# First item's x in whole rows, turned on the tensor engine; the adjacency compared later; the second item's products beside the first attention block

## The chip, the cores and the metric

The kernel runs on one core of a Trainium2 chip. The core has five engines that work side by side, each through its own list of instructions in order: PE (TensorE) multiplies matrices, DVE (VectorE) and POOL (GpSimd) do elementwise work, ACT (ScalarE) does functions and copies, SP issues transfers. Engines wait for one another by semaphores. The metric is device microseconds of one launch. The kernel before took 2934.19 us, the median of 4 runs (2933.64 to 2935.59).

## The reference

x has 32 items of 512 nodes by 512 features; adj is one 512 by 512 matrix of zeros and ones for all items. A masked attention with 8 heads of 64 is followed by a graph convolution, each with a residual and a layer norm:

```python
q, k, v = x @ Wq + bq, x @ Wk + bk, x @ Wv + bv          # per head of 64
scores = q k^T / sqrt(64) + where(adj == 0, -1e9, 0)
x = layernorm(x + softmax(scores) @ v)
norm_adj = adj * rsqrt(deg)[:, None] * rsqrt(deg)[None, :]   # deg = adj.sum(axis=1)
x = layernorm(x + norm_adj @ (x @ weight) + bias)
```

## The kernel before

**Work of one item.** The three products x Wv, x Wk, x Wq need x with its features on the partitions (tile XT). Each product of 2 by 2 blocks is made as seven block products instead of eight (function `seven`, the Winograd scheme): slots 0 to 3 of XT and of a weight tile are the plain blocks, and slots 4, 5, 6 and again 2 are differences or sums of them (`combine` for XT, `weigh` for a weight). A product of seven is called a piece below: PE multiplies a slot of XT with a slot of a weight into one of three PSUM tiles (`mm`, three buffers), and DVE adds it into the result. Pieces of the values come from `values_of(b)` (seven per item), pieces of keys and queries from `keys_and_queries(b, r)` (seven for r = 0, seven for r = 1). Pieces 1 and 2 read slots 0 and 1 of XT, piece 3 slot 5, piece 4 slot 6, piece 5 slot 4, pieces 6 and 7 slots 2 and 3.

**Attention** goes in four blocks per item, a block being two heads. A block has two halves; in each, `scores` multiplies keys and queries (tile sc, two PSUM buffers), DVE caps them and subtracts the mask (e<-sc,maskT), ACT takes the exponential in place, POOL adds the exponentials into acc (`accumulate`). One block later `values` multiplies them with v (tile av), and after every second block `sums` multiplies acc of two blocks with a selecting matrix sel, to get the row sums for all partitions.

**The order of the work is written out by hand.** The class InOrder (line 44, so nearly every instruction of the profile stands on L44) keeps every engine's instructions in the order of the program text. The main loop (line 704) runs over k, the blocks of all items. A turn of it puts out: the additions of acc left over from the block before (`pending`), the first half of the scores of block k, `values` of block k - 1, `sums` where k is even, the second half of the scores, and then one share of the next item's work (`shares`, made by `cut`, which counts pieces). For the first item the shares of k = 1 to 4 are 6, 5, 5 and 5 pieces; `degrees` (row sums of adj and their roots, DVE then POOL) and the four sums and differences of the last weight W1 (`w1_parts`, on POOL) lie between the pieces.

**The start.** x of an item is read in pieces of 32 elements (128 bytes) per row, so that DVE's transposition of 32 by 32 blocks (`turn`, two halves per item) gives XT. SP issues eight such transfers for item 0, then the biases, Wk, Wq, adj and W1; the queue of ACT issues Wv. Then follow the values of item 0 (7 pieces), its keys and queries (14 pieces), and between the last seven of these `adjacency(m)` for four m: PE transposes a block row of adj, and DVE makes the mask from it (maskT), copies it rounded (adjT), compares the two (off) and counts the differences (lost). After that comes `turn(1, 0)`, and the loop starts; the second half of item 1 is turned after the scores of block 0.

Of the kernel before, what the change touches and what calls it, by code (L numbers as in the profile page):

```python
# [9 lines left out]
F32 = mybir.dt.float32  # L10
# [3 lines left out]
AF = mybir.ActivationFunctionType  # L14
ALU = mybir.AluOpType
AX = mybir.AxisListType

P = 128
# [31 lines left out]
def unshifted(  # L50
# [54 lines left out]
    def load_x(b, j):  # L105


        if b == 0 and j == 1:
            X[b, j] = work.tile([P, 8, DT, 32], F32, name="x1", tag="e", bufs=6)
        else:  # L110
            X[b, j] = acts.tile([P, 8, DT, 32], F32, name="x", bufs=1)
        for q in range(4):
            nc.sync.dma_start(
                X[b, j][32 * q : 32 * (q + 1)],
                x[b, ts(j, HALF), ts(q, P)].rearrange("(k s) (t r) -> s k t r", s=32, r=32),
            )

    def turn(b, j):
        vector.transpose(
            XT[:, 2 * j : 2 * j + 2].rearrange("p i u (k s) -> p (i u) k s", s=32),  # L120
            X.pop((b, j)).rearrange("p k t r -> p t k r"),
        )
        if j == 0 and b:
            load_x(b, 1)

    def combine(b, at):
        to, a, c = ((4, 2, 0), (5, 3, 4), (6, 3, 2), (2, 5, 1))[at]
# [15 lines left out]
        for i in range(NT):  # L143
            nc.sync.dma_start(R[b][i], x[b, ts(i, P), :])

    def load_parts(w, name, engine):
        t = consts.tile([P, 7, 2, HALF], F32, name=name)
        for i in range(2):
            for q in range(4):
                engine.dma_start(  # L150
                    t[32 * q : 32 * (q + 1), 2 * i : 2 * i + 2].rearrange("r j u o -> r (j u) o"),
                    w[ts(q, P), ts(i, HALF)].rearrange("(t r) o -> r t o", r=32),
                )
        return t
# [7 lines left out]
    def weigh(t, engine):  # L162
        for at in range(4):
            weigh_part(t, engine, at)

    def load_row(v, name, engine):
        t = consts.tile([P, v.shape[0]], F32, name=name)
        engine.dma_start(t, bass.AP(tensor=v.tensor, offset=v.offset, ap=[[0, P], [1, v.shape[0]]]))
        return t

    def load_column(v, name):
        t = consts.tile([P, DT], F32, name=name)
        nc.sync.dma_start(t, v.rearrange("(t p) -> p t", p=P))
        return t

    load_x(0, 0)
    load_x(0, 1)
    wv = load_parts(Wv, "wv", nc.scalar)
    bv_r = load_row(bv, "bv_r", nc.scalar)
    bk_c = load_column(bk, "bk_c")  # L180
    bq_c = load_column(bq, "bq_c")
    wk = load_parts(Wk, "wk", nc.sync)
    wq = load_parts(Wq, "wq", nc.sync)
    adj_sb = acts.tile([P, NT, N], F32, name="yT")
    nc.sync.dma_start(adj_sb, adj.rearrange("(t p) o -> p t o", p=P))
    w1 = consts.tile([P, 7, 2, HALF], F32, name="w1")
    for i in range(2):
# [2 lines left out]
            W1[:, ts(i, HALF)].rearrange("(t p) o -> p t o", p=P),  # L190
        )
    b1_r = load_row(b1, "b1_r", nc.sync)

    ident = consts.tile([P, P], F32, name="ident")
    make_identity(nc, ident)
# [11 lines left out]
    dis = consts.tile([P, NT], F32, name="dis")  # L207
    lost = consts.tile([P, NT], F32, name="lost")

    def adjacency(m):  # L210


        p = ps_mm.tile([P, N], F32, name="mm")
        for n in range(NT):
            tensor.transpose(p[:, ts(n, P)], adj_sb[:, n, ts(m, P)], ident)
        vector.tensor_scalar(maskT[:, m, :], p, 0.0, FAR, op0=ALU.is_equal, op1=ALU.mult)
        vector.tensor_copy(adjT[:, m, :], p)
        off = work.tile([P, N], F32, name="off", tag="e", bufs=6)
        vector.tensor_tensor(off, p, adjT[:, m, :], ALU.not_equal)
        vector.tensor_reduce(lost[:, m : m + 1], off, AX.X, ALU.add)  # L220

    deg = consts.tile([P, NT], F32, name="deg")
    rdeg = consts.tile([P, NT], F32, name="rdeg")
# [109 lines left out]
    def turns(b):  # L333

        return [(0, turn, (b, 0))], [(0, turn, (b, 1))] + [(0, combine, (b, k)) for k in range(4)]
# [321 lines left out]
    def run(pieces):  # L657
        for _, f, args in pieces:
            f(*args)
# [22 lines left out]
    blocks = [(b, g) for b in range(B) for g in ORDER]  # L682
    S = len(blocks)
    weigh(wv, gpsimd)
    run(sum(turns(0), []))
    weigh(wk, gpsimd)
    scalar.activation(wq[:, :4], wq[:, :4], AF.Copy, scale=SCALE)
    first = values_of(0)
    run(first[:2])
    value_biases()  # L690
    biases()
    if B > 1:
        load_x(1, 0)
    run(first[2:])
    masks = [(0, adjacency, (m,)) for m in range(NT)]
    first = keys_and_queries(0, 0)
    run(first[:1])
    weigh(wq, vector)
    run(first[1:])
    run(weave(masks, keys_and_queries(0, 1)))  # L700
    one, two = turns(1)
    run(one)
# [1 line left out]
    for k in range(S + 1):  # L704
        b, at = divmod(k, G)
        if at == 1:
            if 0 < b < B - 1:
                load_residual(b - 1)
            if b + 2 < B:
                load_x(b + 2, 0)  # L710
            if b + 1 < B:
                main, kq = values_of(b + 1) + keys_and_queries(b + 1, 0), keys_and_queries(b + 1, 1)
                turn0, turn1 = turns(b + 2) if b + 2 < B else ([], [])
                main += kq[:5]
            if b == 0:
                w1_parts = [(0, weigh_part, (w1, gpsimd, i)) for i in range(4)]
                side = main[:7] + [(0, degrees, ())] + weave(w1_parts, main[7:]) + turn0 + kq[5:] + turn1
                shares = cut(side, (6, 5, 5, 5))
            elif b < B - 1:
                f, c = finish(b - 1), convolve(b - 1)  # L720
                norm, split, grow = f["norm"], f["split"], f["grow"]
                add, measure = f["add"], f["measure"]
                put_off = [(0, more, ())]


                beside = {
                    0: rest[:1], 1: rest[1:3], 2: put_off, 3: rest[3:4], 4: rest[4:5] + put_off,
                    5: rest[5:6] + f["inverse"], 6: rest[6:] + add[:2], 7: add[2:],
                    8: measure[:2] + put_off, 9: measure[2:], 10: f["root"] + put_off, 11: norm[:1],
                    12: norm[1:2] + split[:1], 13: norm[2:3] + split[1:2], 14: norm[3:] + split[2:3],  # L730
                    15: split[3:] + f["judge"], 16: put_off + grow[:2], 17: put_off + grow[2:], 18: turn0,
                }
                side = sum(([piece] + beside.get(i, []) for i, piece in enumerate(main)), [])
                side += c["first"] + c["parts"] + kq[5:] + turn1[:1]
                s = c["second"]
                if b < B - 2:
                    side += put_off + s[:1] + put_off + s[1:3] + turn1[1:2] + s[3:4] + turn1[2:3] + s[4:5]
                    side += turn1[3:4] + s[5:6] + c["measure"][:1] + turn1[4:] + s[6:] + c["measure"][1:2]
                    rest = c["measure"][2:] + c["root"] + c["store"]
                    shares = cut(side, (8, 8, 8, 8))  # L740
                else:
                    held, h, last = c, s, finish(b)
                    add = last["add"]
                    side += h[:1] + last["inverse"] + h[1:2] + add[:2] + h[2:3] + add[2:]
                    shares = cut(side, (8, 8, 8, 4))
            else:
                f, c, last = last, convolve(b - 1), finish(b)
                s, first, norm, split, add = c["second"], c["first"], f["norm"], f["split"], last["early"][1:]
                shares = [
                    h[3:4] + f["measure"][:2] + h[6:] + f["measure"][2:] + f["root"] + h[4:5] + f["judge"] + norm[:2]  # L750
                    + h[5:6] + split[:1] + norm[2:] + split[1:2],
                    split[2:] + last["early"][:1] + first[:1] + add[:2] + first[1:2] + add[2:] + first[2:]
                    + c["parts"] + f["grow"],
                    held["measure"] + held["root"] + s[:2] + held["store"],
                    [],
                ]


        while pending:
            more()  # L760
        if k == S - 2:
            load_residual(B - 1)
        if k < S:
            scores((*blocks[k], 0))
        if k:
            values((*blocks[k - 1], 0))
            values((*blocks[k - 1], 1))
            if k % 2 == 0:
                sums(blocks[k - 1][0], (k - 1) % G // 2)
        if k < S:  # L770
            accumulate((*blocks[k], 0))
            scores((*blocks[k], 1))
            if b == B - 1:
                accumulate((*blocks[k], 1))
            else:
                pending += [((*blocks[k], 1), (l,)) for l in range(2)]
        if k == S - G - 1:
            load_residual(B - 2)
        if k == 0:
            run(two)  # L780
        elif shares:
            run(shares.pop(0))

# [309 lines left out]
```

## Time and profile before

The profiled execution took 2933.54 us, its span is 2931.7 us, and the granted PE clock was 0.995 over it.

| | busy us | share |
|---|---|---|
| PE | 2872.2 | 98% |
| PE weight loads (beside PE) | 1882.8 | 64% |
| DVE | 2080.9 | 71% |
| ACT | 1057.2 | 36% |
| POOL | 1811.5 | 62% |

The page gives shares of the whole span. The change lies in the first 140 us, so what matters is read from the rows in order of time: the start, the duration, the engine, what is written from what, and in brackets how long the engine sat idle before it and what ended that. Matmuls overlap, so the step from one start to the next counts, not the duration of one. A float32 product is recorded as two matmuls. On PE the first piece starts at 9.48 us, the first scores at 56.87, and block 5 (the second block of item 1) at 134.10.

### The profile page before, as it was taken

How to read it: one execution, taken by the hardware profiler on the slowest of the kernel's cores; microseconds unless marked ns; L12 is line 12 of the kernel's file. 1: busy time of each engine (PE TensorE's matmuls, PEld its weight loads, DVE VectorE, ACT ScalarE, POOL GpSimd, SP SyncE). 2: the span in 40 equal slices, each digit the busy share in tenths (PEclk: the TensorE clock that was granted, in tenths of full speed). 3: DMA queues.
4: the chain of work that ended last, by engine and by line, in shares of the span. 5: the costliest groups of instructions: out<-in, count | busy, mean ns of one | idle time of the engine just before them, and what ended most of it. 6: DMA issues, size and time to landing. Idle time of an engine off the chain costs nothing.

```text
span 2931.7 us, 35519 instructions
## 1 busy us (share of the span) xinstructions
PE 2872.2 (98%) x12966; PEld 1882.8 (64%) x12966; DVE 2080.9 (71%) x2910; ACT 1057.2 (36%) x1340; POOL 1811.5 (62%) x1141
## 2 busy tenths in 40 slices
PE   7999999999999999999999999999999999999996
PEld 5666666666666666666666666666666666666654
DVE  7677766677666777666776667776667766777667
ACT  1233333343333433333432334333333333343343
POOL 2566666656666666666566666666566666656665
PEclk9999999999999999999999999999999999999998
DMA  5111122112221111211122211212111122111211
GB/s 130 33 26 47 47 58 53 38 37 51 54 54 42 40 49 47 58 42 39 47 51 54 55 40 36 53 49 55 43 40 47 48 57 54 40 37 48 58 33 52
DMA packets 383400, 142.42 MB, mean 49 GB/s; under 512 B 280048, under 2 KB 349680, under 8 KB 383216
## 3 DMA queue, kind: packets, MB, share of 16 engines
q1 hardware_dynamic: 381920, 138.75, 19.8%
q8 instruction: 104, 1.70, 0.2%
q10 hardware_dynamic: 1296, 1.31, 0.2%
q14 instruction: 80, 0.66, 0.1%
HBM read 72.88 MB, written 33.55 MB: 36 GB/s over the span
## 4 chain that ended last, share of the span: by engine, by line
PE 74%; DVE 16%; ACT 6%; issue 2%; POOL 2%; DMA 1%; SPq 0%; DVEq 0%; POOLq 0%; ACTq 0%
PE mm L44 47%; PE sc L44 15%; PE av L44 12%; DVE u L44 3%; ACT yT L44 3%; DVE e L44 3%; DVE st L44 3%; ACT hi L44 2%; DVE lo L44 2%; DVE low L44 1%; POOL rstd L44 1%; ACT e L44 1%; DVE mv L44 1%; DVE kq L44 1%; DVE v L44 1%
## 5 line engine op out<-in xcount | busy, mean ns | idle before, releaser
L44 ACT ACTIVATE e<-e 128x1024 f32<-128x1024 f32 x512 | 540.8, 1057 | 1096.5 <-DVE e L44 1077.8
L44 DVE SCALAR_TENSOR_TENSOR e<-sc,maskT 128x1024 f32<-128x1024 f32 x512 | 600.0, 1212 | 77.4 <-PE sc L44 76.9
L44 POOL TENSOR_TENSOR acc<-acc,e 128x1024 f32<-128x1024 f32 x248 | 597.3, 2408 | 64.3 <-ACT e L44 54.4
L44 PE MATMUL sc<-kq 64*128 64x512 f32 x2048 | 520.4, 622 | 17.1 <-DVE e L44 17.1
L44 POOL TENSOR_TENSOR acc<-e 128x1024 f32<-128x1024 f32 x126 | 296.9, 2356 | 382.3 <-ACT e L44 271.4
L44 PE MATMUL mm<-xT,wk 128*128 128x256 f32 x1792 | 469.6, 384 | 1.0 <-DVE off L44 1.0
L44 PE MATMUL av<-e,v 128*64 128x512 f32 x2048 | 467.7, 598 | 0.0
L44 PE MATMUL mm<-xT,wq 128*128 128x256 f32 x1792 | 459.9, 379 | 0.0
L44 PE MATMUL mm<-wv,xT 128*128 128x256 f32 x1792 | 407.5, 385 | 18.0 <-DVE xT L44 10.6
L44 PEld LDWEIGHTS mm<-xT,wk 128*128 128x128 f32 x1792 | 332.4, 190 | 113.5 <-issue 69.7
L44 PEld LDWEIGHTS mm<-wv,xT 128*128 128x128 f32 x1792 | 338.0, 192 | 93.6 <-issue 26.6
L44 PEld LDWEIGHTS mm<-xT,wq 128*128 128x128 f32 x1792 | 340.5, 190 | 46.3
L44 PEld LDWEIGHTS sc<-kq 64*128 64x128 f32 x2048 | 174.3, 186 | 301.5 <-issue 172.7
L44 PEld LDWEIGHTS av<-e,v 128*64 128x64 f32 x2048 | 135.6, 136 | 315.9 <-issue 315.2
L44 DVE TENSOR_TENSOR kq<-u,mm 128x512 f32<-128x512 f32 x128 | 87.9, 687 | 238.1 <-PE mm L44 238.0
L44 POOL TENSOR_TENSOR yT<-yT,xr 128x512 f32<-128x512 f32 x124 | 193.4, 1588 | 80.6 <-DVE yT L44 80.6
L44 PE MATMUL mm<-w,zT 128*128 128x256 f32 x992 | 224.5, 379 | 0.0
L44 POOL TENSOR_TENSOR rstd<-ve,minus_half 128x4 f32<-128x4 f32 (+1 forms) x65 | 65.5, 1008 | 252.9 <-DVE nmu L44 252.8
L44 POOL TENSOR_TENSOR yT<-yT,b_r 128x512 f32<-128x512 f32 x124 | 170.1, 1381 | 59.6 <-DVE lo L44 59.6
L44 PEld LDWEIGHTS mm<-w,zT 128*128 128x128 f32 x992 | 188.3, 190 | 26.3 <-issue 0.8
L44 PE MATMUL mm<-adjT,hi 128*128 128x512 f32 x496 | 201.9, 407 | 0.0
L44 PE MATMUL mm<-adjT,lo 128*128 128x512 f32 x496 | 196.1, 395 | 0.2 <-DVE lo L44 0.2
(123 smaller groups left out, 3177.7 us busy)
## 6 DMA issues: line engine op xcount, KB each, us to landing
x<-in_x_dram SPq DMA_DIRECT2D x256, 128.0 KB, 2.9
out_dram<-y SPq DMA_DIRECT2D x128, 256.0 KB, 2.1
xr<-in_x_dram SPq DMA_DIRECT2D x124, 256.0 KB, 3.6
yT<-yb SPq DMA_DIRECT2D x496, 64.0 KB, 2.5
wv<-in_L_gnn_Wv_dram ACTq DMA_DIRECT2D x8, 128.0 KB, 4.7
wk<-in_L_gnn_Wk_dram SPq DMA_DIRECT2D x8, 128.0 KB, 4.0
wq<-in_L_gnn_Wq_dram SPq DMA_DIRECT2D x8, 128.0 KB, 4.6
yT<-in_adj_dram SPq DMA_DIRECT2D x1, 1024.0 KB, 6.7
```

The source lines that it names most:

```text
L44: return self.tc.keep_in_program_order(op(*args, **kwargs))
```

## The change

- Item 0 of x is read first, as four transfers of 128 whole rows each (`load_residual(0)`, which was issued after the loads of the next item, at 26.55 us, and is needed later as the residual in any case). `turn_first(j)` makes half of XT from it on PE: 32 float32 products, each of 32 columns of the rows with the identity, into 32 partitions of a scores tile; the copy into XT is split between DVE (first quarter) and ACT (second). DVE's two `turn`s of item 0 and their eight transfers of 128-byte runs are gone.
- The second half of Wv goes on SP's queue behind x, Wk comes before the two bias columns. Both halves of item 1's x are issued before the loop, the second into one of the e buffers.
- Pieces 1 and 2 of the values of item 0 are put beside the turning, then DVE's four `combine`s. The four `weigh` steps of Wq lie between the first pieces of keys and queries.
- `adjacency` keeps only maskT on DVE; ACT copies adjT and an unrounded copy plainT. Comparison and counting (`compare(m)`) move into the shares of k = 3 and 4.
- The second half of item 1 is turned right after the first half of the scores of block 0, and five pieces of item 1's values are put into block 0: two after the first half of the scores, three after the second. The shares of k = 1 to 4 become 4 pieces each, and `degrees` follows the last two pieces of the values, in the share of k = 1.

```diff
+    def turn_first(j):
+        p = ps_sc.tile([P, 2, 2, HALF], F32, name="sc")
+        for i in range(2):
+            for u in range(2):
+                for n in range(2):
+                    for q in range(4):
+                        at = q * P + (2 * i + u) * 32
+                        tensor.matmul(
+                            p[32 * q : 32 * (q + 1), i, u, ts(n, P)], R[0][2 * j + n][:, at : at + 32], ident,
+                            start=True, stop=True,
+                        )
+            (scalar.copy if i else vector.tensor_copy)(XT[:, 2 * j + i], p[:, i])
...
-    load_x(0, 0)
-    load_x(0, 1)
-    wv = load_parts(Wv, "wv", nc.scalar)
+    load_residual(0)
+    wv = load_parts(Wv, "wv", (nc.scalar, nc.sync))
     bv_r = load_row(bv, "bv_r", nc.scalar)
+    wk = load_parts(Wk, "wk", (nc.sync, nc.sync))
     bk_c = load_column(bk, "bk_c")
     bq_c = load_column(bq, "bq_c")
-    wk = load_parts(Wk, "wk", nc.sync)
-    wq = load_parts(Wq, "wq", nc.sync)
+    wq = load_parts(Wq, "wq", (nc.sync, nc.sync))
...
     b1_r = load_row(b1, "b1_r", nc.sync)
+    if B > 1:
+        load_x(1, 0)
+        load_x(1, 1)
...
         vector.tensor_scalar(maskT[:, m, :], p, 0.0, FAR, op0=ALU.is_equal, op1=ALU.mult)
-        vector.tensor_copy(adjT[:, m, :], p)
-        off = work.tile([P, N], F32, name="off", tag="e", bufs=6)
-        vector.tensor_tensor(off, p, adjT[:, m, :], ALU.not_equal)
-        vector.tensor_reduce(lost[:, m : m + 1], off, AX.X, ALU.add)
+        scalar.copy(adjT[:, m, :], p)
+        scalar.copy(plainT[:, m, :], p)
+
+    def compare(m):
+        vector.tensor_tensor(plainT[:, m, :], plainT[:, m, :], adjT[:, m, :], ALU.not_equal)
+        vector.tensor_reduce(lost[:, m : m + 1], plainT[:, m, :], AX.X, ALU.add)
...
     weigh(wv, gpsimd)
-    run(sum(turns(0), []))
     weigh(wk, gpsimd)
-    scalar.activation(wq[:, :4], wq[:, :4], AF.Copy, scale=SCALE)
     first = values_of(0)
-    run(first[:2])
+    turn_first(0)
+    run(first[:1])
+    turn_first(1)
+    run(first[1:2])
+    for k in range(4):
+        combine(0, k)
     value_biases()
     biases()
-    if B > 1:
-        load_x(1, 0)
+    scalar.activation(wq[:, :4], wq[:, :4], AF.Copy, scale=SCALE)
     run(first[2:])
+    wq_parts = [(0, weigh_part, (wq, vector, k)) for k in range(4)]
+    first = keys_and_queries(0, 0)
+    run(wq_parts[:2] + first[:1] + wq_parts[2:3] + first[1:2] + wq_parts[3:] + first[2:])
     masks = [(0, adjacency, (m,)) for m in range(NT)]
-    first = keys_and_queries(0, 0)
-    run(first[:1])
-    weigh(wq, vector)
-    run(first[1:])
     run(weave(masks, keys_and_queries(0, 1)))
...
             if b == 0:
                 w1_parts = [(0, weigh_part, (w1, gpsimd, i)) for i in range(4)]
-                side = main[:7] + [(0, degrees, ())] + weave(w1_parts, main[7:]) + turn0 + kq[5:] + turn1
-                shares = cut(side, (6, 5, 5, 5))
+                exact = [(0, compare, (m,)) for m in range(NT)]
+                side = early[5:] + [(0, degrees, ())] + weave(w1_parts + exact, main) + turn0 + kq[5:] + turn1
+                shares = cut(side, (4, 4, 4, 4))
...
         if k < S:
             scores((*blocks[k], 0))
+        if k == 0:
+            run(two)
+            early = values_of(1)
+            run(early[:2])
...
         if k == 0:
-            run(two)
+            run(early[2:5])
         elif shares:
             run(shares.pop(0))
```

More of the change, by code (lines that the diff above doesn't have):

```diff
@@ L105, in load_x @@
     def load_x(b, j):
-        if b == 0 and j == 1:
+        if b == 1 and j == 1:
             X[b, j] = work.tile([P, 8, DT, 32], F32, name="x1", tag="e", bufs=6)
@@ L122, in turn @@
         )
-        if j == 0 and b:
+        if j == 0 and b > 1:
             load_x(b, 1)
+    def turn_first(j):
[10 more added lines that the diff above has]
+            (scalar.copy if i else vector.tensor_copy)(XT[:, 2 * j + i], p[:, i])
     def combine(b, at):
@@ L144, in load_residual, with load_parts @@
             nc.sync.dma_start(R[b][i], x[b, ts(i, P), :])
-    def load_parts(w, name, engine):
+    def load_parts(w, name, engines):
         t = consts.tile([P, 7, 2, HALF], F32, name=name)
@@ L149, in load_parts @@
             for q in range(4):
-                engine.dma_start(
+                engines[i].dma_start(
                     t[32 * q : 32 * (q + 1), 2 * i : 2 * i + 2].rearrange("r j u o -> r (j u) o"),
@@ L208, in unshifted @@
     lost = consts.tile([P, NT], F32, name="lost")
+    plainT = acts.tile([P, NT, N], F32, name="plainT", tag="hi", bufs=1)
     def adjacency(m):
@@ L706, in unshifted @@
         if at == 1:
-            if 0 < b < B - 1:
+            if 1 < b < B - 1:
                 load_residual(b - 1)
@@ L711, in unshifted @@
             if b + 1 < B:
-                main, kq = values_of(b + 1) + keys_and_queries(b + 1, 0), keys_and_queries(b + 1, 1)
+                main, kq = keys_and_queries(b + 1, 0), keys_and_queries(b + 1, 1)
+                if b:
+                    main = values_of(b + 1) + main
                 turn0, turn1 = turns(b + 2) if b + 2 < B else ([], [])
```

## The prediction

> **What bounds the kernel now.** The page first: PE is busy for 98% of the span and leads the chain, so time is lost only where PE waits or runs at a lower clock.
>
> ```profile
> span 2931.7 us, 35519 instructions
> PE 2872.2 (98%) x12966; PEld 1882.8 (64%) x12966; DVE 2080.9 (71%) x2910; ACT 1057.2 (36%) x1340; POOL 1811.5 (62%) x1141
> PE 74%; DVE 16%; ACT 6%; issue 2%; POOL 2%; DMA 1%; SPq 0%; DVEq 0%; POOLq 0%; ACTq 0%
> ```
>
> Then the timeline to 110 us, where the change lies. The reader is to see PE's starts and the gaps between them: transfers and DVE end the first ones, DVE those at 54.98 and 61.70.
>
> ```profile
> 8.18 1.25 DVE L44 STREAM_TRANSPOSE xT<-x 128x1024 f32<-128x1024 f32 x1 [8.18 <-DMA x<-in_x_dram]
> 9.48 6.27 PE L44 MATMUL mm<-wv,xT 128*128 128x256 f32 x16 [9.48 <-DVE xT L44]
> 12.70 1.25 DVE L44 STREAM_TRANSPOSE xT<-x 128x1024 f32<-128x1024 f32 x1 [3.27 <-DMA x<-in_x_dram]
> 13.98 6.08 DVE L44 TENSOR_TENSOR xT<-xT 128x512 f32<-128x512 f32 x4
> 16.86 1.97 PE L44 MATMUL mm<-wv,xT 128*128 128x256 f32 x8 [1.12 <-DVE xT L44]
> 20.81 8.86 PE L44 MATMUL mm<-wv,xT 128*128 128x256 f32 x32 [1.98 <-DVE e L44]
> 54.98 1.10 PE L44 MATMUL mm<-xT,wk 128*128 128x256 f32 x4 [0.97 <-DVE off L44]
> 61.70 5.66 PE L44 MATMUL sc<-kq 64*128 64x512 f32 x16 [2.84 <-DVE e L44]
> 72.80 10.63 PE L44 MATMUL mm<-wv,xT 128*128 128x256 f32 x48
> ```
>
> Next the windows of that stretch: after the idle times the granted clock falls.
>
> ```profile
> 15.00:30.00 15.00, 11.90 (x47) 9.48 (x46) 14.24 (x17) 3.19 (x2) 10.04 (x7) 0.89 1.11 285
> 22.00:23.00 1.00, 1.00 (x4) 0.50 1.15 236
> 60.00:75.00 15.00, 13.30 (x50) 5.46 (x51) 11.86 (x12) 7.88 (x8) 9.72 (x6) 0.89 0.35 83
> ```
>
> Last the timeline from 80 us, for POOL in front of the sums:
>
> ```profile
> 79.84 5.12 POOL L44 TENSOR_TENSOR acc<-acc,e 128x1024 f32<-128x1024 f32 x2
> 88.86 0.16 PEld L44 LDWEIGHTS mm<-acc,sel 128*32 128x32 f32 x8 [0.81 <-issue]
> 88.86 1.06 PE L44 MATMUL mm<-acc,sel 128*32 128x512 f32 x8
> 94.41 2.28 DVE L44 TENSOR_REDUCE deg<-yT 128x4 f32<-128x2048 f32 x1
> 96.97 1.02 POOL L44 TENSOR_TENSOR dis<-safe,minus_half 128x4 f32<-128x4 f32 x1 [4.54 <-DVE safe L44]
> 97.96 1.01 POOL L44 TENSOR_TENSOR rdeg<-safe,half 128x4 f32<-128x4 f32 x1
> 98.94 1.27 POOL L44 TENSOR_TENSOR w<-w 128x512 f32<-128x512 f32 x1
> 100.17 4.80 POOL L44 TENSOR_TENSOR acc<-acc,e 128x1024 f32<-128x1024 f32 x2
> ```
>
> **Prices on PE**, by steps between starts: a piece 1.73 us (eight recorded matmuls of 0.216), half a block's scores 1.92, its values 3.58, sums 0.99, the transposes of one mask 0.43. With them PE's work up to block 5 (134.10) is 42 pieces, 4 masks, 5 blocks of scores, 4 of values, 2 sums: 110 us. The other 24 are lost: 9.5 before the first piece; 7.9 from there to 29.50, when keys begin (20.0 for 12.1 of work); 1.4 beside the masks (27.4 for 26.0); 4.7 from the first scores to 72.80 (15.9 for 11.3); 0.7 after that. From block 5 on the instructions of every engine stand in the same order in both programs, so only these 24 us, and what is added to them, can move.
>
> **1. The rows of x.** SP issues two transfers of 256 KB first, at 0.74 and 1.19. Transfers of this shape land 3.6 us after issue (page, xr), so both by 4.8 at best; I take 4.9. The far bound is 8.05, when the first half of x landed before. Half of Wv moves from ACT's queue to SP's, behind x, and Wk ahead of the small biases. Cover: POOL began on Wv at 13.23 and had slot 5 some 3 us later, while piece 3 now starts only at about 21. Wq and adj, needed at 29 and 43, were issued by 20 and move by a few issues of about 0.5 us. Item 1's second half (four issues of 0.4 us) goes ahead of nothing that is awaited.
>
> **2. Turning on PE.** Each half is 64 recorded matmuls of 128 columns into 32 partitions, four of them in a row into different partitions. Nearest row: sums, eight such matmuls of 512 columns, step 0.99, where one alone steps 0.43: four run at once. A matmul of 128 columns steps 0.108, so a half is 16 x 0.108 = 1.7 us, or 3.4 at half clock. One by one it would be 6.9 and 13.8; I take four at once, the same output shape. In the program the second quarter of each half also waits for DVE's copy of the first (0.69 as other copies out of PSUM, with 0.35 to get there and back): 1.05 each. Chain: 4.9 + 1.7 (half clock) + 1.05 + 1.7 = 9.4; piece 1, partly at half clock (before, PE got full clock about 5 us after it started), 3.0: 12.4; turning 0.9 + 1.05 + 0.9: 15.2; piece 2: 17.0; DVE's addition 0.9: 17.8. Only then come DVE's combinations (13.98 before). Piece 3 needs two of them at 1.52, beside POOL's Wk: 20.85. Five pieces, 8.65: 29.5. PE has idled 3.9 us by then, and after 1.98 us it ran at 0.50 for some 3.2 us, so 1.6 more; and DVE's four small steps on the biases (21.37 to 25.22, stretched by POOL), now in front of the first drain, hold a PSUM buffer up to 0.9 us, I take 0.4. Keys begin at 31.5 instead of 29.5: **+2.0**, from -0.5 (no fall of the clock) to +4.5 (rows at 6.4, slow piece 1); one by one is a rival below. ACT's table load (1.28) and its two copies lie beside these.
>
> [...]
>
> **3. Masks.** DVE loses a cast, a comparison and a reduction per mask (4 x 2.06 us), ACT gains eight copies of 0.58 in a stretch where it is nearly idle. The wait of 0.97 at 54.98 goes; next late is the chain mask, adjT, plainT (2.2 us) before a PSUM buffer comes free, against 2.16 of PE work at the last mask. **-1.2** (-1.4 to -0.8).
>
> **4. Block 0.** Before: idle 2.84, then half clock. Now, counted from the first score: turn(1, 0) 1.0 to 2.25; scores end at 1.92, piece 1 waits 0.4; pieces 1 and 2 to 5.8; second scores to 7.7; turn(1, 1) waits for two e (1.16 each), ends 5.75, POOL's two combinations (1.3 each) 8.4, piece 3 waits 0.75. Three pieces end at 13.65: 1.15 lost instead of 4.7. POOL's additions to acc now stand behind the four combinations, which costs nothing: the e ring asks for them at 20. **-3.5** (-4.2 to -2.6).
>
> **5. POOL in front of the first sums.** Here a wait is added. Sums at k = 2 need acc of block 1. Before, POOL had it at 84.96, 3.9 us ahead of the sums. Now the degrees and two steps on W1 lie in the share of k = 1, and in POOL's order dis, rdeg, W1, W1 stand ahead of these two additions. From PE's start on the piece behind the last value piece (93.60 before): 5.34 to POOL's W1 (98.94), two of them 2.54, additions 4.80: 12.7 us. PE in that time has two pieces, half a block's scores and values: 8.96. PE stands 3.75 us, everything on it behind the sums; the clock then falls as above, 1.6. **+5.4** (+3.0 if DVE's reduction is quicker and the clock stays, to +7).
>
> **6. Comparing later.** The step before item 2's first turn, on DVE, is compare(3): 1.5 beside POOL (u+bias took 2.02, an uncontended step 0.65) and 0.69 for the reduction, less 0.85 of idle time there. That makes turn(2, 0) 1.3 late, and so SP's load of the other half, which took 4.6 us to reach DVE (133.22 to 137.83), turn(2, 1), the e behind it and PE, which waited 0.57 there already. **+1.3** (0 to +3). The other three comparisons lie under PE's pieces, with three PSUM buffers in hand.
>
> **Sum.** +2.0 - 1.2 - 3.5 + 5.4 + 1.3 = +4.0. On the profiled execution (2933.54; 1.84 of it lies around the span) 2937.5, and the median stands 0.65 above that: 2938.2.
>
> **Rivals.** *A, turning is one by one* (slower). For: every product brings a new stationary block, which no row of before shows at this rate. Against: the sums. Price: 128 matmuls, 23 of them at half clock, 13.8 + 2.4 instead of 5.1: +11, so 2949. It decides (over 2940.1) once a half takes 1 us longer than I take. *B, the sums don't wait* (towards faster). For: before, they had 3.9 us of slack. Against: the order of POOL. Price: the sum without 5.4, 2932.8, and 2929 to 2931 with the start at its low end. *C, the rows land no earlier*: the load of Wv runs beside them, and the DMA share of the first 15 us was 0.99. Against: 128-byte runs moved some 200 GB/s, rows of 2 KB 320 to 380. Price: rows at 8.05, +3.1: 2941.3.
>
> **How the numbers follow.** Within 0.2% (5.9 us) a measurement of this kernel can't tell a change from none; it ends at 2928.3 and 2940.1. My forecast has 0.54 (0.14 slower, 0.40 same), A 0.16 (slower), B 0.18 (0.07 faster, 0.11 same), C 0.12 (0.07 slower, 0.05 same). The terms' own bounds that go together give 2931 to 2946; the range reaches 2931 to 2947, leaving out most of A and the low end of B.
>
> **What would show it.** PE's first matmul near 5 us, sc<-ident in groups of four; values of item 0 ending near 31; no idle PE at 55 and under 1.5 us in block 0; at the first sums PE idle 3 to 4 us, released by POOL, then a lower clock; at block 5 a wait for DVE of 1.5 to 2. Wrong if the turning steps 0.1 per matmul, if POOL is done before the sums, or if anything after block 5 differs.

## The result, and the profile after

The changed kernel took 2938.42 us, the median of 40 executions, where the kernel before took 2934.2 (60 executions, 2932.79 to 2936.18). The ratio is 1.0014, with a 95% interval of 1.001 to 1.0019: slower by 4.2 us, and within the 0.2% that the prediction counts as no change. One of the 40 executions took 7395.37 us and is left out of the ratio; the others lie between 2935.87 and 2941.31. The kernel ends in a guard (`bad > 0`) behind which a second, general program stands; whether it was taken there, and how long it takes, no run shows. No other kernel here had such an execution, and its cause stays open.

The profiled execution took 2938.73 us. Its page, in the lines that answer to those of before (span; busy time of each engine):

```profile
span 2936.9 us, 35770 instructions
PE 2876.8 (98%) x13094; PEld 1886.2 (64%) x13094; DVE 2074.5 (71%) x2906; ACT 1063.2 (36%) x1350; POOL 1812.4 (62%) x1141
```

PE has 128 matmuls more, the turning of item 0, and its busy time grew by 4.6 us. As before, the page can't say where the time went. The timeline can; these are rows picked from it in order of time (start, duration, engine, tiles, and the idle time before with what ended it). First four rows of the kernel before, where keys begin, where the scores begin, and at block 5:

```profile
29.50 1.03 PE L44 MATMUL mm<-xT,wk 128*128 128x256 f32 x4
56.87 1.99 PE L44 MATMUL sc<-kq 64*128 64x512 f32 x8
140.24 2.26 PE L44 MATMUL sc<-kq 64*128 64x512 f32 x8 [0.57 <-DVE e L44]
153.92 1.97 PE L44 MATMUL mm<-wv,xT 128*128 128x256 f32 x8 [0.43 <-DVE e L44]
```

The changed kernel:

```profile
4.68 0.65 PE L44 MATMUL sc<-ident,xr 128*32 128x128 f32 x8 [4.68 <-DMA xr<-in_x_dram]
6.05 1.51 PE L44 MATMUL sc<-ident,xr 128*32 128x128 f32 x24 [0.73 <-DMA xr<-in_x_dram]
8.38 1.93 PE L44 MATMUL sc<-ident,xr 128*32 128x128 f32 x32 [0.81 <-DVE xT L44]
10.24 3.78 PE L44 MATMUL mm<-wv,xT 128*128 128x256 f32 x8
13.95 0.81 PEld L44 LDWEIGHTS sc<-ident,xr 128*32 128x32 f32 x32 [0.65 <-issue]
13.95 1.08 PE L44 MATMUL sc<-ident,xr 128*32 128x128 f32 x32
19.49 5.54 DVE L44 TENSOR_TENSOR xT<-xT 128x512 f32<-128x512 f32 x4
22.78 10.56 PE L44 MATMUL mm<-wv,xT 128*128 128x256 f32 x40 [3.93 <-DVE xT L44]
33.17 1.03 PE L44 MATMUL mm<-xT,wk 128*128 128x256 f32 x4
...
57.88 1.13 PE L44 MATMUL mm<-xT,wk 128*128 128x256 f32 x4 [0.34 <-DVE kq L44]
59.80 1.99 PE L44 MATMUL sc<-kq 64*128 64x512 f32 x8
67.96 5.45 PE L44 MATMUL mm<-wv,xT 128*128 128x256 f32 x24 [0.45 <-POOL xT L44]
73.34 1.99 PE L44 MATMUL sc<-kq 64*128 64x512 f32 x8
...
87.69 1.02 POOL L44 TENSOR_TENSOR dis<-safe,minus_half 128x4 f32<-128x4 f32 x1 [7.15 <-DVE safe L44]
89.66 2.64 POOL L44 TENSOR_TENSOR w<-w 128x512 f32<-128x512 f32 x2
92.26 4.77 POOL L44 TENSOR_TENSOR acc<-acc,e 128x1024 f32<-128x1024 f32 x2
93.37 1.05 PE L44 MATMUL mm<-acc,sel 128*32 128x512 f32 x4
97.08 1.05 PE L44 MATMUL mm<-acc,sel 128*32 128x512 f32 x4 [2.66 <-POOL acc L44]
98.06 1.99 PE L44 MATMUL sc<-kq 64*128 64x512 f32 x8
...
143.68 2.26 PE L44 MATMUL sc<-kq 64*128 64x512 f32 x8 [0.98 <-DVE e L44]
157.38 1.97 PE L44 MATMUL mm<-wv,xT 128*128 128x256 f32 x8 [0.45 <-DVE e L44]
```

Read down PE's starts. Rows of x let PE start at 4.68 instead of 9.48, yet keys begin at 33.17 instead of 29.50. The last wait beside the masks (0.97 at 54.98) has become 0.34. Block 0 has 0.45 us of idle time in place of 2.84. The sums, one step of 0.99 before, are cut in two by POOL: the second four start at 97.08 only, and POOL's rows show why, with the roots of the degrees and two steps on W1 ahead of the additions to acc. At block 5 PE waits 0.98 where it waited 0.57. The next wait for DVE, 0.45 at 157.38, stood in the kernel before too (0.43 at 153.92).

As a sum of differences, by those starts: +3.67 to the keys; -0.74 from there to the first scores (26.63 against 27.37); +3.70 at the first sums (a step of 4.69 against 0.99); +0.41 at block 5; and, since PE is only 3.44 later behind that wait (143.68 against 140.24), -3.60 in block 0 and the rest. Read directly, block 0 gives the same: from its first scores to those of block 1 the changed kernel takes 13.54 for 12.49 of work at the prediction's prices (1.05 lost), and the kernel before took 15.93, up to item 1's first piece, for 11.26 (4.67 lost). From block 6 on both programs keep the same pace; the difference of their starts creeps from 3.46 (162.92 against 159.46) to 3.75 over 120 blocks, and the last 90 us of this pair of executions add 1.44 more, in instructions that are the same. In the kernels below, with the same instructions there, that last stretch lies between 0.4 shorter and 2.4 longer than in the profile of before, so it isn't put down to the change; what moves it is open.

The windows of the changed kernel (stretch, length, busy time and count of PE, PEld, DVE, ACT and POOL, granted clock of PE, DMA share, GB/s):

```profile
10.00:15.00 5.00, 5.00 (x48) 3.34 (x40) 0.69 (x1) 0.59 (x1) 2.27 (x2) 1.00 1.12 220
24.00:28.00 4.00, 4.00 (x13) 3.21 (x12) 2.24 (x7) 1.36 (x1) 0.00 (x0) 0.57 1.08 366
95.00:100.00 5.00, 2.92 (x13) 0.85 (x13) 0.69 (x1) 0.59 (x1) 5.00 (x3) 1.00 0.37 52
```

After the idle time of 3.93 at 22.78 the clock falls, as predicted: 0.57 from 24 to 28. After the wait in the sums it does not: 1.00. And piece 1, between 10 and 14, took 3.78 for eight matmuls that take 1.99 later, under a clock printed as 1.00. That 1.00 is no reading: the trace's records of the clock begin at 13.96, where the full rate begins, and a window without a record prints 1.00.

### The profile page after: what moved, and what is told of

It reads as the page before. It is cut to its first block, busy times and chain, and to the rows that moved or that the text cites. A ratio compares the mean times of both kernels' runs of the same rounds, so it can differ in the third digit from the quotient of the medians.

```text
span 2936.9 us, 35770 instructions
## 1 busy us (share of the span) xinstructions
PE 2876.8 (98%) x13094; PEld 1886.2 (64%) x13094; DVE 2074.5 (71%) x2906; ACT 1063.2 (36%) x1350; POOL 1812.4 (62%) x1141
## 4 chain that ended last, share of the span: by engine, by line
PE 73%; DVE 16%; ACT 6%; POOL 2%; issue 2%; DMA 0%; SPq 0%; DVEq 0%; POOLq 0%; ACTq 0%
PE mm L44 47%; PE sc L44 15%; PE av L44 11%; DVE u L44 3%; ACT yT L44 3%; DVE e L44 3%; DVE st L44 3%; ACT hi L44 2%; DVE lo L44 2%; DVE low L44 1%; POOL rstd L44 1%; ACT e L44 1%; DVE mv L44 1%; DVE v L44 1%; DVE kq L44 1%
```

## The experiments

My theory: two waits that the change brings cost what block 0 and the masks give back, the start (about +3.7) and POOL in front of the first sums (+3.7, and sometimes a slower clock). The rivals: the time is lost elsewhere, so that undoing either part changes nothing; or the turning is serial.

**POOL's order undone.** The degrees and the steps on W1 go behind the additions to acc of block 1; the comparisons keep their order and get fixed places.

```diff
-                side = early[5:] + [(0, degrees, ())] + weave(w1_parts + exact, main) + turn0 + kq[5:] + turn1
+                at_piece = {3: [(0, degrees, ())], 4: w1_parts[:1], 5: w1_parts[1:2], 6: w1_parts[2:3],
+                            7: w1_parts[3:] + exact[:1], 8: exact[1:2], 10: exact[2:3], 11: exact[3:]}
+                side = early[5:] + sum((at_piece.get(i, []) + [piece] for i, piece in enumerate(main)), [])
+                side += turn0 + kq[5:] + turn1
```

> Only POOL's order and the place of the degrees change: the degrees follow the third piece of item 1's keys and queries, and the four steps on W1 follow later pieces, so that the additions to acc of block 1 stand ahead of them on POOL. If the wait of PE at the first sums (3.70 us between the two halves of the sums and the next scores, where 0.99 was) is a full loss, it goes and the time falls by 3.7 us, to 2934.7. If the loss is made good later anyway, because PE catches up or because POOL's work is only late at the next sums (k = 4), the time stays at 2938.4 or falls by less than 1.

Measured: 2934.18 us (11 executions, 2932.7 to 2935.98), ratio to before 0.9998, interval 0.9989 to 1.0007. The timeline of this kernel:

```profile
92.75 1.06 PE L44 MATMUL mm<-acc,sel 128*32 128x512 f32 x8
100.87 1.02 POOL L44 TENSOR_TENSOR dis<-safe,minus_half 128x4 f32<-128x4 f32 x1 [4.55 <-DVE safe L44]
```

All eight matmuls of the sums follow one another again, and POOL takes the roots 13 us later than in the changed kernel (100.87 against 87.69), where nobody waits. The medians lie 4.2 us apart, as much as the whole loss of the change. 3.70 of it is the wait in the trace; the comparisons in their fixed places move block 5's wait by 0.09 only (0.89).

**The old start with the rest of the change.** Item 0's x comes in 128-byte runs and is turned by DVE again, with the loads and the steps on Wq about where they were before; masks, block 0, sums and comparisons stay as changed.

```diff
-    load_residual(0)
-    wv = load_parts(Wv, "wv", (nc.scalar, nc.sync))
+    load_x(0, 0)
+    load_x(0, 1)
+    wv = load_parts(Wv, "wv", (nc.scalar, nc.scalar))
...
+    run(sum(turns(0), []))
     weigh(wk, gpsimd)
...
-    turn_first(0)
-    run(first[:1])
-    turn_first(1)
-    run(first[1:2])
-    for k in range(4):
-        combine(0, k)
+    run(first[:2])
```

> The start of before (x in runs of 128 bytes, turned on DVE, loads and combinations in the order of before) with all the rest of the change. If the start is what costs 3.7 us (keys begin at 33.17 instead of 29.50), keys begin at 29.5 again and the time is 2934.7. If turning on PE only shifts the loss (the transfers or the clock would take it in any case), it stays at 2938.4.

Measured: 2935.54 us (11 executions, 2934.37 to 2938.39), ratio 1.0005, 0.9996 to 1.0014. Keys begin at 29.44, 3.73 earlier than in the changed kernel, and the time falls by 2.9. In the profiled execution the clock takes a part of the gain back, at the sums:

```profile
93.34 1.49 PE L44 MATMUL mm<-acc,sel 128*32 128x512 f32 x4 [2.66 <-POOL acc L44]
94.76 3.19 PE L44 MATMUL sc<-kq 64*128 64x512 f32 x8
```

and its window there (columns as above):

```profile
95.00:100.00 5.00, 5.00 (x18) 2.84 (x19) 2.44 (x3) 2.11 (x3) 3.73 (x4) 0.78 0.00 0
```

The wait is the same 2.66 us as in the changed kernel, but here scores take 3.19 instead of 1.99: 0.45 us in the sums and 1.21 up to the next keys, 1.66 in all.

**Both undone.** The two edits together; what is left of the change are the masks, block 0 and the later comparisons.

```diff
-    load_residual(0)
+    load_x(0, 0)
+    load_x(0, 1)
...
-                side = early[5:] + [(0, degrees, ())] + weave(w1_parts + exact, main) + turn0 + kq[5:] + turn1
+                side = early[5:] + sum((at_piece.get(i, []) + [piece] for i, piece in enumerate(main)), [])
+                side += turn0 + kq[5:] + turn1
```

> The start of before and POOL's work late, so that only the masks, block 0 and the later comparison remain of the change. If the parts add up (-0.7 masks, -3.6 block 0, +0.4 at block 5), it is 3.9 below before: 2930.3. If block 0's gain was tied to the new start (item 1's x loaded early, a free DVE), it is between 2932 and 2934.

Measured: 2930.72 us (11 executions, 2929.91 to 2931.41), ratio 0.9989, 0.998 to 0.9998. With the three kernels above this makes a square:

| median, us | POOL in front of the sums | POOL behind them | difference |
|---|---|---|---|
| new start | 2938.42 | 2934.18 | 4.24 |
| old start | 2935.54 | 2930.72 | 4.82 |
| difference | 2.88 | 3.46 | |

The two costs add up, in either order, within the scatter of the executions (the two differences of a row or column lie 0.6 apart), and what remains of the change (2930.72 against 2934.2) is worth 3.5 us. The theory holds; that the loss lies elsewhere is ruled out.

**Turning in one column group at a time.** The loop over q, the four groups of 32 partitions, moves outward, so that neighbouring products write the same partitions.

```diff
         for i in range(2):
-            for u in range(2):
-                for n in range(2):
-                    for q in range(4):
+            for q in range(4):
+                for u in range(2):
+                    for n in range(2):
```

> The turning matmuls in another order: 8 recorded matmuls into the same 32 partitions follow one another, where the partitions changed with each product. If four ran at once because neighbours wrote into different partitions, a quarter (32 matmuls) takes 3.5 us at full clock where it took 0.87 to 1.1, keys begin 7 to 8 us later (41) and the time is 2946. If the step of 0.03 us has another cause, such as short weight loads of 32 columns, nothing changes: 2938.4.

Measured: 2940.8 us (one execution). PE's rows of it:

```profile
10.66 2.46 PE L44 MATMUL sc<-ident,xr 128*32 128x128 f32 x32 [0.78 <-DVE xT L44]
13.05 1.99 PE L44 MATMUL mm<-wv,xT 128*128 128x256 f32 x8
24.88 8.87 PE L44 MATMUL mm<-wv,xT 128*128 128x256 f32 x40 [2.27 <-DVE xT L44]
33.59 1.03 PE L44 MATMUL mm<-xT,wk 128*128 128x256 f32 x4
98.48 3.56 PE L44 MATMUL sc<-kq 64*128 64x512 f32 x8
```

A quarter of 32 matmuls steps 2.39 here (10.66 to 13.05), 0.075 each; in the changed kernel it steps about 1.0 (15.84 to 16.86), 0.032 each. So the changed kernel does run them side by side, and its order of loops matters. But neither expectation held on the time: keys come only 0.42 later than in the changed kernel, not 8. PE, busy for longer at the start (4.07 from 5.81 on, not 1.51 from 6.05), ran piece 1 at full rate (1.99, not 3.78), and after 2.27 us of idle time the clock didn't fall in front of piece 3 (8.87, not 10.56). Of the rest of its +2.4, 1.65 is a fall of the clock after the sums, as in the kernel with the old start.

**A longer wait at the sums.** Two more steps of POOL on W1 ahead of the additions. They repeat the first of the four sums and differences.

```diff
+        if k == 2:
+            weigh_part(w1, gpsimd, 0)
+            weigh_part(w1, gpsimd, 0)
         while pending:
             more()
```

> Two more steps on POOL (W1's first sum twice more, 1.27 us each, same values) ahead of the additions that the first sums wait for. PE then idles 5.2 us instead of 2.66. If every us of POOL there is a us of the end, the time rises by 2.5, to 2940.9, and the granted clock stays at 1.00. If an idle time of this length lowers the clock, as I had expected of the shorter one, the row behind it shows a granted clock of about 0.5 for some 3 us, and the time rises by 4.1, to 2942.5.

Measured: 2945.54 us (one execution), 7.1 above the changed kernel. PE's rows:

```profile
100.23 1.92 PE L44 MATMUL mm<-acc,sel 128*32 128x512 f32 x4 [5.35 <-POOL acc L44]
102.08 3.78 PE L44 MATMUL sc<-kq 64*128 64x512 f32 x8
```

Its window after the wait:

```profile
100.00:106.00 6.00, 5.77 (x13) 1.57 (x14) 1.31 (x2) 1.05 (x2) 4.97 (x4) 0.50 0.00 0
```

PE's wait grows by 2.69 (2.66 to 5.35), one for one with POOL's two steps of 1.3: POOL's order sets the sums. The clock then stands at 0.50 from 99.50 to 106.33, which costs 2.9 more (0.87 in the sums, 2.04 in the scores and the first keys behind them), above the 1.6 that I had allowed for a fall. The other 1.5 of the 7.1 lie elsewhere: keys begin 0.48 later in this execution, and its last 90 us are 1.0 longer.

**Without the comparisons.** The four comparisons and counts are left out, and the count is set to zero.

```diff
-                exact = [(0, compare, (m,)) for m in range(NT)]
+                exact = []
+                vector.memset(lost, 0.0)
```

> The changed kernel without the four comparisons and reductions (the count of differences is set to zero: that part of the computation is left out). If compare(3) in front of the turn of item 2 is what lengthens the wait at block 5 (0.98 idle where 0.57 was), that wait is back at about 0.6 or less and the time falls by 0.4, to 2938.0. If the comparisons also hold PE elsewhere through the PSUM buffers, it falls by 1 or more.

The edit moves POOL's work as well: without the comparisons to share the places with, only one step on W1 instead of two stands ahead of the additions to acc.

Measured: 2939.05 us (one execution). At the sums and at block 5 this kernel has

```profile
98.73 1.05 PE L44 MATMUL mm<-acc,sel 128*32 128x512 f32 x4 [1.32 <-POOL acc L44]
144.92 2.26 PE L44 MATMUL sc<-kq 64*128 64x512 f32 x8 [0.57 <-DVE e L44]
```

The second row is the wait of before to the hundredth, and with all comparisons, but made earlier, it is 0.47 (the last experiment below). So 0.41 of the changed kernel's 0.98 is the doing of the late comparison. The wait of 0.45 at 157.38 is gone too, and from the values of block 4 to those of block 12 it takes 180.48 instead of 181.27; but the kernel before had that second wait without a comparison near it, and took 180.82, so it isn't a cost of comparing later. The first row is a second proof of POOL's part: with one, two and four steps on W1 ahead of the additions PE waits 1.32, 2.66 and 5.35. The time as a whole says little, because the sums wait 1.34 less and keys began at 36.17 in this execution: Wv came later (PE waited 1.14 for it, where in the changed kernel its weight load waited 0.38), and five pieces took 11.89 at a lower clock (0.50 from 24 to 30). The start of the changed kernel scatters; in the four executions profiled with it keys begin at 32.56, 33.17, 33.65 and 36.17.

**PE kept busy from the start.** Eight products of the identity with itself (16 recorded matmuls) ahead of the rows of x, their results unused.

```diff
     first = values_of(0)
+    p = ps_mm.tile([P, N], F32, name="mm")
+    for _ in range(8):
+        tensor.matmul(p[:, :P], ident, ident, start=True, stop=True)
     turn_first(0)
```

> The changed kernel with eight products of the identity with itself on PE ahead of the rows of x, from about 1.4 to 4.8 us, results unused. Theory: the start came out 1.7 us later than predicted because PE ran the second half of the first turning (1.93 us where 0.87 is its work), and all of piece 1 (3.78 instead of 1.8), at half clock. With the clock up sooner piece 1 begins near 9 and takes about 2, the combinations begin near 16.5 instead of 19.5, piece 3 near 19.7 instead of 22.8, and keys near 30 instead of 33.2: about 2935.3. Rival: the first microseconds are bound by the rows landing (6.05), by the weights of the values and by DVE, and the clock only fills that: keys between 32.5 and 33.2 again, 2938.4.

Measured: 2936.08 us (11 executions, 2933.9 to 2938.75), ratio to before 1.0006, 0.9997 to 1.0015. PE's rows:

```profile
1.36 3.78 PE L44 MATMUL mm<-ident 128*128 128x128 f32 x16 [1.36 <-POOL ident masks.py:199]
9.65 1.99 PE L44 MATMUL mm<-wv,xT 128*128 128x256 f32 x8 [0.79 <-DMA wv<-in_L_gnn_Wv_dram]
19.61 10.56 PE L44 MATMUL mm<-wv,xT 128*128 128x256 f32 x40 [3.14 <-DVE xT L44]
30.01 1.03 PE L44 MATMUL mm<-xT,wk 128*128 128x256 f32 x4
```

Two of its windows, ahead of the keys and after the sums:

```profile
20.00:25.00 5.00, 5.00 (x17) 4.11 (x16) 4.93 (x7) 1.91 (x1) 3.86 (x3) 0.66 1.00 311
95.00:100.00 5.00, 5.00 (x15) 2.54 (x16) 2.45 (x2) 2.08 (x3) 4.67 (x4) 0.66 0.01 2
```

Piece 1 takes 1.99, and keys begin at 30.01, 3.16 earlier, as the theory had it. So most of the late start, 3.16 of 3.67, is the half rate of PE's first microseconds (3.78 for piece 1), not the transfers. The median gains 2.3 of that, since Wv now holds piece 1 for 0.79 and the profiled execution has the clock fall twice, in front of piece 3 and, unlike the changed kernel's, after the sums.

**Both halves turned first.** The halves no longer share one PSUM tile, DVE's combinations come before it takes pieces 1 and 2, ACT scales Wq in two parts, and POOL's order is the late one.

```diff
         for i in range(2):
+            p = ps_mm.tile([P, 2, HALF], F32, name="mm") if j else ps_sc.tile([P, 2, HALF], F32, name="sc")
...
     turn_first(0)
-    run(first[:1])
     turn_first(1)
-    run(first[1:2])
     for k in range(4):
         combine(0, k)
+    run(first[:2])
```

> Both halves of x are turned before any piece, each quarter into a PSUM tile of its own (so PE does not wait for DVE's copy in between), DVE makes the combinations before it drains pieces 1 and 2, Wq is scaled in two halves, and POOL's work is late as in the first experiment. If the late start came from the combinations standing behind pieces 1 and 2 and their drains (they began at 19.49 there), piece 3 waits only for POOL's Wv (12.65 + 2.6), keys begin at about 25.5, limited by Wq's transfer (landed at 23.45), and with the sums free the time is 2938.4 - 7.7 - 3.7 = 2927.0, less than both kernels. If the transfers or the low clock set the start, keys stay near 32 and the time is 2934.5.

Measured: 2927.6 us (11 executions, 2926.38 to 2929.4), ratio 0.9977, 0.9968 to 0.9986. Keys begin at 26.98. What is left of waits, in the timeline:

```profile
11.64 3.82 DVE L44 TENSOR_TENSOR xT<-xT 128x512 f32<-128x512 f32 x4
16.64 5.45 PE L44 MATMUL mm<-wv,xT 128*128 128x256 f32 x24 [1.28 <-POOL wv L44]
19.86 1.17 DVE L44 COPY bias<-bk_c 128x4 f32<-128x4 f32 x1 [1.76 <-DMA bk_c<-in_L_gnn_bk_dram]
23.02 3.72 PE L44 MATMUL mm<-wv,xT 128*128 128x256 f32 x16 [0.93 <-DVE e L44]
```

The combinations begin 7.85 earlier than in the changed kernel, and now POOL's work on Wv is late, then DVE, which stands 1.76 us for a small transfer with pieces to take behind it.

**The bias columns later, the comparisons earlier.** The same kernel with those two edits:

```diff
     value_biases()
-    biases()
...
     run(first[2:])
+    biases()
...
+                at_piece = {3: [(0, degrees, ())], 4: w1_parts[:1] + exact[:1], 5: w1_parts[1:2],
+                            6: w1_parts[2:3] + exact[1:2], 7: w1_parts[3:] + exact[2:3], 9: exact[3:]}
```

> As e7_turn_both_first, with the four small steps on the bias columns (they waited 1.76 us for their transfer there, and held DVE with it) put behind the values, and the comparisons one to two pieces earlier, so that the last is not in front of item 2's first turning. Theory (what is left of the start and of block 5 is these waits of DVE): piece 6 of the values starts without its 0.93 us of idle time, keys near 26.0 instead of 27.0, block 5's wait back to 0.57 from 0.85, in all 2926.2 where that kernel had 2927.6. Rival: values wait for POOL on Wv or for Wq in its place, 2927.6, or the comparisons run beside other DVE work and make the shares of block 3 late, over 2928.

Measured: 2925.13 us (6 executions, 2924.92 to 2926.09), ratio 0.9969, 0.9957 to 0.9981: 9.0 us below before, the best kernel here. PE's rows:

```profile
16.02 8.90 PE L44 MATMUL mm<-wv,xT 128*128 128x256 f32 x40 [1.63 <-POOL wv L44]
24.76 1.03 PE L44 MATMUL mm<-xT,wk 128*128 128x256 f32 x4
131.05 2.26 PE L44 MATMUL sc<-kq 64*128 64x512 f32 x8 [0.47 <-DVE e L44]
```

Five pieces run without a stall and without a fall of the clock, and block 5's wait is 0.47. PE now waits 1.63 for POOL on Wv, the next thing late at the start.

## Why the prediction was right, and where its terms were off

The time came out at 2938.42 against 2938.2, and no measurable change, on the slow side, was the likeliest outcome named. Step by step, the signs were all right. The sizes were not: the start cost 1.7 more and the masks gave 0.5 less than the sum had, the sums cost 1.7 less and the later comparison 0.9 less. That these four errors cancel to within 0.6 is luck, and so is a total that is right to 0.2.

- **The start** was the term most mis-sized: +3.67 measured, +2.0 in the sum. Its chain can be compared entry by entry. The step "4.9 + 1.7 (half clock) + 1.05 + 1.7 = 9.4" held for the first of the two transfers (4.68) but not for the second: PE had its rows at 6.05, and piece 1 started at 10.24 (+0.84). "Piece 1, partly at half clock, 3.0" was 3.71, all of it at half rate (+0.71). DVE's two combinations in front of piece 3 took 3.29 against 3.05 (+0.24). Turning the second half, 2.91 against 2.85, and the fall of the clock in front of the keys (10.39 for five pieces, 10.65 with the fall and the PSUM wait that the prediction allowed) held. The kernel with PE kept busy confirms the reading of piece 1: with piece 1 and half of the first turning at full rate, keys begin 0.5 us after those of before.
- **Masks**: -0.74, predicted -1.2. PE waits 0.34 at 57.88 for DVE's step into kq, a wait that I had put at nothing; I had looked at the chain of mask and copies only.
- **Block 0**: from its first scores to those of block 1, with its second scores and five pieces between, 13.54; predicted 13.65. -3.60 against -3.5.
- **POOL in front of the sums**: the wait was 3.70, predicted 3.75, from the same order of instructions. The fall of the clock, 1.6 in the sum, is absent in the profile of the changed kernel and is 1.66 after the same idle time in the kernel with the old start; two more of the profiled kernels with that wait of 2.66 (serial turning, and PE kept busy) show about 1.65 as well. So the term is +3.7 or about +5.35, and the sum had taken the higher for certain. How often the changed kernel itself pays the fall isn't shown, since one execution of it was profiled.
- **Comparing later**: +0.41, predicted +1.3, both at block 5. The step "1.5 beside POOL" failed: the fourth comparison ran at 0.69, with POOL idle beside it. The first two, at 117.14 and 119.84, did take 2.06 and 2.12, where nothing waited for them.
- **Rival A** fell by mechanism, since four run at once, and its price was wrong as well: 0.075 per matmul instead of 0.108, and with piece 1 at full rate (1.99) and no fall of the clock in front of piece 3 (8.87 for five pieces) keys came only 0.42 later. **Rival B** fell: the sums wait, and undoing it gives 2934.18, not 2932.8, since the start is late as well. **Rival C** was half right: a part of the rows landed later than 4.9, but at 6.05, not 8.05.

The weight loads of the turning ran beside its matmuls: the 32 of a quarter lie within 0.81 us (13.95 in the changed kernel), under matmuls that last 1.08, all on 128 rows.

The sum of what was measured, +3.67 - 0.74 - 3.60 + 3.70 + 0.41, is +3.44, where the prediction had +4.0 on the trace; the medians differ by 4.2. The 0.8 in between is less than what the last 90 us (1.44 in this pair) and a fall of the clock (1.65) move from one execution to another; which of them it is isn't shown. Two of the signs that the prediction named did not show: a lower clock behind the first sums, and a wait of 1.5 to 2 at block 5.

## What to carry to other kernels

When work is moved between shares of an in-order engine, look at what stands next on that engine's queue and who waits for it: here four small steps of POOL, put ahead of the additions that the sums need, cost 4.2 us, more than the 3.5 that masks, block 0 and the later comparison won together, and moving them back cost nothing. An early first instruction is worth little if the chain behind it has round trips: put all that feeds the chain (both turnings, then the combinations) ahead of the work that only fills, and count PE's first microseconds at half rate (here 3.78 for eight matmuls that later took 1.99). A small transfer can hold an engine as long as a big one does, if its consumer stands in front of what PE needs: the 2 KB of bk landed 5.3 us after issue in the kernel before, the pieces of Wk, 128 KB each, after 4.0.

## What the runs showed of the hardware that was not expected

- In the first 9 us after its first matmul (4.68 to 13.95 in the changed kernel) PE ran at about half rate: eight matmuls in 3.78 at 10.24, and 32 of the turning in 1.93 at 8.38 but 1.08 at 13.95. With PE busy from 1.36 on, the same steps took 1.99 and 1.08 from 7.78. The windows print 1.00 for that time, for want of a record: in the changed kernel's trace the records of the clock begin with the full rate, at 13.96.
- After an idle time of 2.66 at the same place of the program, the clock fell in three profiled executions (about 1.65 us lost in each) and not in a fourth, the changed kernel (1.00 from 95 to 100); after 5.35 us it fell, and longer (0.50 from 99.50 to 106.33, 2.9 lost). Before piece 3, it fell after 1.98 (0.50 from 22 to 24 in the kernel before), 3.14 and 3.93 (five pieces in 10.56), and not after 2.27 and 1.63 (8.87 and 8.90). The length of the gap alone doesn't decide.
- In the traces of before and after, every change of the clock lies a whole number of steps of 3.413 us behind the first record (14.66 and 13.96). Over the first 2800 us of these two, steps at full clock with 1.98, 2.67 (before) and 1.99 us (after) of idle time ended in a fall of one step; one with 1.94, from 17.37 to 20.79 in the changed kernel, and those with up to 1.46 did not. The 2.66 at the sums of the changed kernel was split by the end of a step, 1.46 and 1.20. That the place of a gap among these steps counts beside its length is my reading of these few falls; no run here moved a gap for that alone.
- Products of 32 columns into the same 32 partitions stepped 0.075 us (serial turning, 10.66 to 13.05), into four different ones 0.032 (changed kernel, 15.84 to 16.86).
- Two steps of DVE on four numbers per partition took 1.17 and 1.23 us beside POOL in the kernel that turns both halves first, and 0.16 each without POOL in the changed kernel; a third, between them, took 0.16 in both.
